# Reordering the border between the first 1x1 convolution and the Winograd 3x3 convolution of a bottleneck block

## The chip, the cores and the metric

The kernel runs on one core of one Trainium2 chip. The metric is the device time of one execution in microseconds; lower is better. All data are fp32.

## The reference

Two ResNet bottleneck blocks run one after the other on `x` of shape (64, 1024, 14, 14). A batch norm takes its mean and variance over the whole batch, so no normalised value exists before the last image of a convolution is done.

```python
def block(x, w1, ..., residual_scale):            # P = 256, Cout = 1024
    out = relu(bn(conv1x1(x, w1) + b1, g1, be1))   # 1024 -> 256
    out = relu(bn(conv3x3(out, w2) + b2, g2, be2)) # 256 -> 256, padding 1
    out = bn(conv1x1(out, w3) + b3, g3, be3)       # 256 -> 1024
    return relu(x + softplus(residual_scale) * out)
y = block(block(x, layer 0 weights), layer 1 weights)
```

## The kernel before, in words

`y_all` holds the 256 channels of the middle of a block in SBUF as two **slots** of 128 channels, for all 12544 pixels. The images are handled in 32 tiles `t` of two images (392 pixels).

**First convolution.** `Conv1` (L336) makes one unit of two tiles (in block 0) or of one tile (in block 1) as a Strassen-Winograd product: seven products `p1` to `p7` of four matmuls each instead of eight. The helper `matmul` (L171) issues every matmul in program order. `stream` (L303) interleaves the products of two consecutive units: `p1` of a unit, then `p4` and `p3` that are left over of the unit before, `p6`, `p5`, `p7`, and `p2`. Slot 1 of a unit is complete after its `p4` and `p7`, slot 0 after its `p2` and `p3`. Each result gets its bias and its `bn_stats` (L388, L391). In block 1 these products alternate with those of block 0's last convolution (`fused`, L1287).

**The border.** After the last `p4`, `one_done` (L1396) aggregates the statistics of slot 1, works out scale and shift in `affine` (L1345, a chain of small VectorE operations round one square root on ScalarE), and normalises slot 1 of the first image group on ScalarE (`norm`, L547). After the last `p3` the same is done for slot 0 (`first_norm`, L940). Then the 3x3 convolution may begin.

**3x3 convolution.** `conv2` (L557) works on 8 groups of 8 images, in one dimension as a Winograd transform with six products per group: pairs (1, 2), (3, 4) and (5, 0). `Inputs` (L603) makes the inputs of a pair on VectorE: row combinations `r` (L594, L683, L689, from a scratch tile `steps`, L700), then `sums` (L625), `v` (L631, with two edge columns on ScalarE, L636 and L637) and `diffs` (L641). Each of the 48 products needs three kinds of matmul, each of four instructions: `m` from `sums` and the filter `ua`, `l` from `diffs` and `ub`, and `columns` from `v` and `ub`, twice. `start` (L749) copies `m` from PSUM into the two halves EVEN and ODD of a `columns` bank pair on ScalarE (L759, L761), on which the `columns` matmuls accumulate; `middle` (L763) copies `l` as `ls` (L772, L774). VectorE adds both as `f` (L801). There are two `columns` pairs, two `l` and two `m` banks. The very first product has no `m` phase: its `sums` matmuls go straight into `columns`, slot 1 first.

The filters `ua` and `ub` are read from DRAM on SyncE's queue (L652). All tiles of `conv2` lie where tiles of the first convolution lay, and a pool waits for all that was in its place before.

The order within SyncE, VectorE and ScalarE is that of the tile scheduler, except where `keep_in_program_order` fixes it. All matmuls and all `act(...)` calls are so fixed; the edge columns, `ls` and the copies into `columns` are not.

The entry to the 3x3 convolution is in the code:

```python
        for banks in (columns(), columns()):
            n = MS * RT * GI * WH
            for q in (ODD, EVEN):
                matmul(banks[:, q, :n], ident, ident[:, :1].to_broadcast([P, n]), start=True, stop=True)
```

Those four matmuls multiply by the identity; nothing reads their result.

## Time and profile before

| | us |
|---|---|
| median of 3 executions (1924.05 to 1924.71) | 1924.67 |
| profiled execution | 1923.4 |
| its span, from first to last instruction | 1921.6 |
| TensorE matmul busy in it | 1903.4 (99%) |
| VectorE busy | 1546.8 (80%) |
| ScalarE busy | 1083.9 (56%) |
| GpSimd busy | 565.1 (29%) |

The profile is of one execution. In the timelines PE stands for TensorE, PEld for its weight loads, DVE for VectorE, ACT for ScalarE, POOL for GpSimd and SP for SyncE. Ends of matmuls are modelled, so the difference of two starts is a better duration than the one that is printed. An fp32 matmul appears as two records, so four matmuls are "x8". In a timeline line the columns are start, duration, engine, source line, operation, output and inputs, count, and in brackets the idle time before it with the instruction that ended it.

### The profile page before, as it was taken

What the parts mean: (1) busy time and instruction counts of PE and PEld (TensorE: products, weight loads), DVE (VectorE), ACT (ScalarE), POOL (GpSimd) and SP (SyncE); (2) the same over time, 40 slices, a digit from 0 to 9 for tenths busy, and PEclk for the clock granted to TensorE, in tenths of its full rate; (3) what the DMA queues carried; (4) which work ended last, traced back from release to release, by engine and by line L of the source; (5) the groups of instructions that cost most, each with busy time, mean ns of one, the idle gap of its engine ahead of it and who ended that gap; (6) DMA issues with size and microseconds to landing.
All of it is one profiled execution on the core that took longest, in us unless ns stands there. A gap on an engine that the chain in (4) does not pass through costs nothing.

```text
span 1921.6 us, 28727 instructions
## 1 busy us (share of the span) xinstructions
PE 1903.4 (99%) x10240; PEld 1597.4 (83%) x10240; DVE 1546.8 (80%) x2491; ACT 1083.9 (56%) x2148; POOL 565.1 (29%) x678
## 2 busy tenths in 40 slices
PE   9999999999999999999999999999999999999999
PEld 5555557999998799999999999989999987555555
DVE  5787767999998866776776767689999986888886
ACT  2222214677778355555555555556777682666665
POOL 0111100211204143433433333302121041666664
PEclk9999999999999999999999999999999999999999
DMA  7777644787856544444444444258778466889998
GB/s 286 271 251 274 220 153 142 199 225 211 211 178 170 189 161 171 169 168 176 179 182 168 168 168 177 125 166 208 222 208 223 142 171 242 290 326 346 325 344 300
DMA packets 198463, 408.77 MB, mean 213 GB/s; under 512 B 37040, under 2 KB 174960, under 8 KB 181808
## 3 DMA queue, kind: packets, MB, share of 16 engines
q1 hardware_dynamic: 159648, 321.84, 48.9%
q0 software_dynamic: 33056, 34.03, 8.6%
q10 hardware_dynamic: 5616, 51.06, 6.4%
q8 instruction: 81, 1.33, 0.3%
q14 instruction: 62, 0.51, 0.1%
HBM read 263.75 MB, written 115.34 MB: 197 GB/s over the span
## 4 chain that ended last, share of the span: by engine, by line
PE 92%; DVE 3%; DMA 1%; issue 1%; POOL 1%; ACT 1%; SPq 0%; DVEq 0%; ACTq 0%; POOLq 0%
PE cy L171 18%; PE ay L171 17%; PE columns L171 13%; PE cp L171 11%; PE ap L171 10%; PE m L171 7%; PE l L171 6%; PE cx L171 5%; PE ax L171 5%; PE ps L171 1%; DMA home<-y 1%; POOL home L1065 1%; DMA x<-in_x 0%; DVE v L631 0%; DVE sums L625 0%
## 5 line engine op out<-in xcount | busy, mean ns | idle before, releaser
L334 ACT ACTIVATE cu<-cy,scale 128x196 f32<-128x196 f32 (+1 forms) x552 | 256.3, 473 | 278.3 <-PE cy L171 272.9
L171 PE MATMUL columns<-v,ub 128*128 128x224 f32 (+1 forms) x1536 | 300.7, 337 | 0.0
L334 ACT ACTIVATE x<-x,shift 128x392 f32<-128x392 f32 x452 | 255.0, 613 | 72.6 <-POOL x L493 53.5
L171 PEld LDWEIGHTS columns<-v,ub 128*128 128x128 f32 x1536 | 269.3, 188 | 2.8
L467 DVE SCALAR_TENSOR_TENSOR x<-cp,scale,x 128x196 f32<-128x196 f32 (+1 forms) x368 | 178.1, 484 | 97.9 <-PE cp L171 96.5
L171 PE MATMUL cy<-ct,ws 128*128 128x196 f32 (+1 forms) x736 | 221.8, 383 | 1.2 <-ACT cu L334 1.2
L488 POOL TENSOR_TENSOR x<-x,cu 128x196 f32<-128x196 f32 (+1 forms) x184 | 159.9, 869 | 171.6 <-ACT cu L334 163.7
L171 PE MATMUL ay<-at,ws 128*128 128x196 f32 (+1 forms) x752 | 209.1, 381 | 0.0
L493 POOL TENSOR_TENSOR x<-x,cu 128x392 f32<-128x392 f32 x124 | 125.9, 1015 | 191.4 <-DVE x L467 191.4
L171 PEld LDWEIGHTS ay<-at,ws 128*128 128x128 f32 x752 | 136.5, 190 | 33.4
L171 PEld LDWEIGHTS cy<-ct,ws 128*128 128x128 f32 x736 | 133.4, 190 | 36.4 <-ACT cu L334 3.9
L171 PE MATMUL l<-diffs,ub 128*128 128x224 f32 (+1 forms) x768 | 149.1, 337 | 2.6 <-PE columns L171 2.6
L514 POOL TENSOR_TENSOR x<-x,cu 128x392 f32<-128x392 f32 x120 | 121.9, 1016 | 86.2 <-DVE x L467 65.3
L171 PE MATMUL m<-sums,ua 128*128 128x224 f32 (+1 forms) x752 | 145.9, 337 | 1.1 <-DVE sums L625 1.1
L334 ACT ACTIVATE au<-ay 128x196 f32<-128x196 f32 (+1 forms) x141 | 53.6, 380 | 155.4 <-PE ay L171 152.6
L171 PEld LDWEIGHTS l<-diffs,ub 128*128 128x128 f32 x768 | 134.3, 189 | 4.4 <-PE columns L171 3.9
L467 DVE SCALAR_TENSOR_TENSOR x<-cx,scale,x 128x196 f32<-128x196 f32 (+1 forms) x184 | 89.1, 484 | 56.7 <-PE cx L171 56.7
L171 PEld LDWEIGHTS m<-sums,ua 128*128 128x128 f32 x752 | 131.3, 189 | 2.9 <-DVE sums L625 2.5
L171 PE MATMUL cy<-y,w 128*128 128x196 f32 (+1 forms) x408 | 125.3, 393 | 0.0
L171 PE MATMUL cx<-y,w 128*128 128x196 f32 (+1 forms) x400 | 122.6, 391 | 0.0
L171 PE MATMUL cp<-y,ws 128*128 128x196 f32 (+1 forms) x368 | 113.6, 390 | 0.0
L761 ACT ACTIVATE columns<-m 128x448 f32<-128x448 f32 (+1 forms) x160 | 78.5, 490 | 59.5 <-PE m L171 57.0
(221 smaller groups left out, 3950.6 us busy)
## 6 DMA issues: line engine op xcount, KB each, us to landing
x<-in_x SPq DMA_DIRECT2D x62, 1568.0 KB, 6.8
ub<-u SPq DMA_DIRECT2D x94, 768.0 KB, 5.5
x<-mid SPq DMA_DIRECT2D x32, 1568.0 KB, 8.1
mid<-x ACTq DMA_DIRECT2D x31, 1568.0 KB, 5.1
out<-x SPq DMA_DIRECT2D x123, 392.0 KB, 5.5
ua<-u SPq DMA_DIRECT2D x94, 256.0 KB, 3.3
u<-y POOLq DMA_DIRECT2D x48, 256.0 KB, 5.6
home<-y SPq DMA_DIRECT2D x70, 96.0 KB, 3.7
```

The source lines that it names most:

```text
L171: tc.keep_in_program_order(nc.tensor.matmul(*args, **kw))
L334: tc.keep_in_program_order(nc.scalar.activation(*args, **kw))
L467: nc.vector.scalar_tensor_tensor(v, bank, self.scale[:, o : o + 1], v, ALU.mult, ALU.add)
L488: nc.gpsimd.tensor_add(self.part(1, 1), self.part(1, 1), u3)
L493: nc.gpsimd.tensor_add(v, v, self.u12)
L514: nc.gpsimd.tensor_add(v, v, self.u12[:, i * self.n : (i + 1) * self.n])
L761: nc.scalar.activation(v, m, AF.Copy)
L1065: ins = queue.dma_start(out=x[32 * i : 32 * i + 32, :, j], in_=y_all[32 * j : 32 * j + 32, :, a + i * run : a + i * run + run])
```

## The change

Four things are done at both borders. In the new code `late` is true in block 0, whose units have two tiles.

1. **The last `Conv1` unit gets an order of its own** (`closing`). `p4` of the last unit moves ahead of its `p2` and, in block 0, of the previous unit's `p3`. Both results of slot 1 then come earlier, and `p2` and `p3` of slot 0 come last. The last unit's `p5` bank is taken from the `ay` pair, its second saved product from another buffer. The summary of earlier statistics is made for each slot by itself.
2. **Slot 1's combinations begin before slot 0 is done.** `conv2` becomes a generator; `Border` advances it between the last products. The inputs of the first pair are made for each slot by itself (`first_combination`), nine small VectorE operations per slot, some of them placed inside slot 0's `affine` (`between`).
3. **The first matmuls are those of two products, slot 1 first**: the first product's `sums`, `l`, and `v`, then the second product's `m` and `l`, all for slot 1, then the same for slot 0. Two of the four identity matmuls are left.
4. **Buffers.** The x tiles are split into two pools of two, one of them on the right side of SBUF. That one is closed at the border, and a pool `early` takes its place for the first `r`, `v`, `sums`, `diffs` and `fa`. The first `ua` and `ub` get slots of their own, in block 0 over `at1` and `at2`, in block 1 over `w3`. The pools at the border and the PSUM pools wait for single tiles (`reuse_waits="tile"`). The loads of the second product's filters are split by slot.

`affine` loses one operation in the chain for one slot.

```diff
+        def closing(self, before):
...
+            yield from self.p1()
+            yield from before.p4()
+            summary(1)
+            if not late:
+                yield from before.p3()
+                summary(0)
+            yield from self.p6()
+            yield from self.p5()
+            yield from self.p7()
+            yield from self.p4()
+            border.affine_of(1)
+            border.norm(1)
+            if late:
+                yield from before.p3()
+                summary(0)
+            border.begin()
+            if late:
+                border.steps(1)
+            yield from self.p2()
+            if late:
+                border.steps(2)
+            yield from self.p3()
+            border.affine_of(0, lambda: border.steps(1 if late else 3))
+            border.norm(0)
+            border.steps(5 if late else 6)
...
-    def conv2(psum, pool, b, par, aff, affine_of, stats):
+    def conv2(b, par, aff, early, rest):
...
-        for banks in (columns(), columns()):
-            n = MS * RT * GI * WH
-            for q in (ODD, EVEN):
-                matmul(banks[:, q, :n], ident, ident[:, :1].to_broadcast([P, n]), start=True, stop=True)
...
+        def first_combination(x, s, t):
...
+            act(t[:, RT - 1], y_all[:, s, GPX - 2 * LINE : GPX], AF.Copy, scale=-3.0)
+            run(stt(t[:, :full], two_rows(0, s)[:, :, 0], -4.0, two_rows(0, s)[:, :, 1]))
+            yield
+            run(nc.vector.tensor_add(ra, t1, t2))
+            yield
+            x.add_columns(slice(0, 1), here)
+            yield
+            first, second = x.subtract_columns, x.step_columns
+            if s == 0:
+                first, second = second, first
+            first(slice(0, 1), here)
+            yield
+            second(slice(0, 1), here)
+            yield
+            run(nc.vector.tensor_sub(rb, t1, t2))
+            yield
+            x.add_columns(slice(1, 2), here)
+            yield
+            x.subtract_columns(slice(1, 2), here)
+            yield
+            x.step_columns(slice(1, 2), here)
+            yield
...
+        both_columns = EVEN, ODD
+        first.open()
+        second.open()
+        l, m, l2 = first.bank("l"), second.bank("m"), second.bank("l")
+        for s in reversed(range(MS)):
+            first.columns(*both_columns, slots=[s], sums=True)
+            if s:
+                first.part(l, DIFF, first.diffs, s)
+
+                n = MS * second.n
+                for q in both_columns:
+                    v = second.banks[:, q].rearrange("p o n -> p (o n)")
+                    matmul(v, ident, ident[:, :1].to_broadcast([P, n]), start=True, stop=True)
+            first.columns(*both_columns, slots=[s])
+            if s == 0:
+                first.part(l, DIFF, first.diffs, s)
+                first.middle(l)
+            second.part(m, SUM, second.sums, s)
+            if s == 0:
+                second.put(m)
+                long_work(0, 0)
+                finished.send(first)
+            second.part(l2, DIFF, second.diffs, s)
...
-        run(nc.vector.tensor_scalar(v, mv[:, :, 1], EPS, None, ALU.add))
+        run(nc.vector.tensor_scalar(v, mv[:, :, 1], EPS, -0.5, ALU.add, ALU.mult))
...
+        between()
         run(nc.vector.reciprocal(r, sd))
...
+                run(nc.vector.scalar_tensor_tensor(q[:, one], v[:, one], r[:, one], r[:, one], ALU.mult, ALU.mult))
+            run(nc.vector.tensor_mul(rg, r, par[:, g : g + n]))
```

## The prediction, put on record before the changed kernel ran

> **What bounds the kernel now.** I read the busy line of the page first, then TensorE's timeline for every gap, then VectorE and ScalarE round the gaps.

> ```profile
> PE 1903.4 (99%) x10240; PEld 1597.4 (83%) x10240; DVE 1546.8 (80%) x2491; ACT 1083.9 (56%) x2148; POOL 565.1 (29%) x678
> ```

> TensorE is busy for all but 18 us of the span, so only its gaps, and matmuls that do nothing, can be won. TensorE at the border of block 0, and the waits that follow:

> ```profile
> 301.45 2.80 PE L171 MATMUL ap<-x,ws 128*128 128x392 f32 x8
> 305.16 3.26 PE L171 MATMUL columns<-ident 128*128 128x448 f32 x8 [0.91 <-DVE y L388]
> 309.45 1.75 PE L171 MATMUL columns<-sums,ua 128*128 128x224 f32 x8 [1.03 <-issue]
> ...
> 320.16 1.69 PE L171 MATMUL columns<-v,ub 128*128 128x224 f32 x8
> 322.24 1.41 PE L171 MATMUL m<-sums,ua 128*128 128x168 f32 x8 [0.39 <-DVE sums L625]
> ...
> 347.80 1.75 PE L171 MATMUL l<-diffs,ub 128*128 128x224 f32 x8 [0.91 <-PE columns L171]
> ...
> 378.73 1.78 PE L171 MATMUL m<-sums,ua 128*128 128x224 f32 x8 [0.22 <-DVE sums L625]
> ...
> 382.45 1.75 PE L171 MATMUL l<-diffs,ub 128*128 128x224 f32 x8 [0.41 <-PE columns L171]
> ```

> The last product of the first convolution starts at 301.45 and, at 2.64 a product, ends at 304.1. The first useful matmul starts at 309.45: 5.3 us, of which 3.26 are identity matmuls. Then 0.39 + 0.91 + 0.22 + 0.41 = 1.93 us of waits follow, all on VectorE (the `diffs` before 347.80 and 382.45 end at 347.70 and 382.35); after that TensorE never waits again in this convolution. Block 1:

> ```profile
> 1255.46 1.49 PE L171 MATMUL ap<-x,ws 128*128 128x196 f32 x8
> 1258.77 3.26 PE L171 MATMUL columns<-ident 128*128 128x448 f32 x8 [1.82 <-DVE y L388]
> 1263.44 1.75 PE L171 MATMUL columns<-sums,ua 128*128 128x224 f32 x8 [1.42 <-issue]
> ...
> 1276.12 1.41 PE L171 MATMUL m<-sums,ua 128*128 128x168 f32 x8 [0.28 <-DVE sums L625]
> ```

> 6.7 us here, and later 0.28, 0.91, 0.21 and 0.41. VectorE in windows:

> ```profile
> 304.00:340.00 36.00, 33.67 (x182) 31.11 (x182) 34.68 (x51) 21.67 (x47) 0.14 (x2) 1.00 0.66 212
> 340.00:380.00 40.00, 38.87 (x220) 37.95 (x219) 38.72 (x50) 25.54 (x51) 6.41 (x6) 1.00 0.78 207
> ```

> The third number after the window's length is VectorE: 73.4 of 76 us. So **for 78 us after the border VectorE paces TensorE**; what TensorE wins at the border is kept only as far as VectorE is early too.

> ```profile
> 304.39 0.62 DVE L388 SCALAR_TENSOR_TENSOR y<-ap,par,au 128x392 f32<-128x392 f32 x1
> ...
> 309.73 0.85 DVE L594 SCALAR_TENSOR_TENSOR steps<-y 128x672 f32<-128x672 f32 x1
> ...
> 315.73 2.95 DVE L700 TENSOR_TENSOR steps<-y 128x2688 f32<-128x2688 f32 x1
> 318.79 1.63 DVE L594 SCALAR_TENSOR_TENSOR r<-steps 128x672 f32<-128x672 f32 x2
> ```

> and ScalarE, where the order of three rows will matter:

> ```profile
> 317.33 1.46 ACT L772 ACTIVATE ls<-l,par 128x224 f32<-128x224 f32 x4 [3.02 <-PE l L171]
> 318.84 1.09 ACT L761 ACTIVATE columns<-m 128x448 f32<-128x448 f32 x2
> 320.45 0.38 ACT L636 ACTIVATE v<-r 128x96 f32<-128x96 f32 x1 [0.52 <-DVE r L594]
> ```

> [...] in block 1 the result L388 of the last product ran only at 1258.20, after slot 1's whole `affine`, though its product ended at 1256.8. [...] for 224 and 448 elements, the rows show 0.39 and 0.62, so halving an operation costs something. [...] SyncE indeed stood until 305.09 for L388, and the first filter loads landed 2.3 us (`ua`, 128 KB) and 4.6 us (`ub`, 384 KB) later.

> **The change, part by part.** Durations are distances of starts in the trace before; orders are those in which the changed kernel's instructions stand on each engine.

> *Identity matmuls*: four become two, 1.63 us less per border, but the two left stand between useful ones and are no longer hidden.

> *Block 0, slot 1.* `p4` moves from 298.82 to 293.55, so slot 1's `affine` ends near 299.0 (5.27 earlier, and one operation of 0.19 less) and its normalisation (1.69) near 300.7. VectorE then does the previous unit's result and summary to 301.2, and `stt` (0.96), `r` (0.66) and `sums` (0.31) of slot 1 between the results of `p2` and `p3`. `sums` is ready at 304.45, so useful matmuls start at 304.55 instead of 309.45. The statistics chain of slot 0 hangs on `p3`, whose end doesn't move.

> *Block 0, VectorE after `p3`.* Of its work 0.96 + 0.66 + 0.31 = 1.93 us was done before; `diffs` fills the wait for the root (0.29); `affine` saves 0.19; the split costs about 0.08 each on four pairs and 0.31 on `r` (1.01 becomes 2 x 0.66), 0.6 in all. So L700 starts 1.9 us earlier (313.8), and the two `r` after it end at 318.5 instead of 320.4.

> *Block 0, TensorE.* From 304.55: `sums` 1.52, a wait for `diffs` to 306.5, `l` 0.76, identity 1.63, `v` 1.52, `m` 0.76, `l` 0.76, then slot 0 (its `sums` ready at 311.4) 1.52 + 1.52 + 0.76 + 0.76 + 0.76: done at 317.25. Next come the second product's EVEN matmuls, which need `columns<-m` from ScalarE. There **the two edge copies of the third product (128x96) now stand ahead of `ls` x4 and `columns<-m`**, and they need both `r` of 318.5. So 318.5 + 0.6 + 1.46 + 0.55 gives 321.2: TensorE waits 3.9 us, EVEN ends at 322.75, and the third product's `m` starts there, against 322.24 before: 0.5 later. `p3` to `m` contains the same 32 useful matmuls in both.

> *Block 0, afterwards.* The waits of 0.91, 0.22 and 0.41 were on VectorE, which is now 1.9 us early; its `diffs` before 347.7 also moves ahead of `fc` and the row outputs. They vanish: 1.54 - 0.5 = **1.0 us won**.

> *Block 1.* Products take 1.33. `p4` moves one product forward only, so `stt`, `r` and `sums` of slot 1 fall inside slot 0's `affine`, where they fill 0.52 of waiting; slot 0's shift comes at 1261.07 (before 1261.01). `sums` of slot 1 is ready at 1260.56 instead of 1263.23, L700 starts at 1268.2 (1.4 earlier). TensorE from 1260.65 by the same lengths: 1272.95. Here `ls` and the first `columns<-m` stand ahead of the edge copies: 1271.45 + 1.5 + 0.55 gives EVEN at 1273.6 and the third `m` at 1275.15, 0.97 earlier. At 1301.7 and 1332.6 VectorE decides: **1.4 us won**.

> *Edits at nothing.* The x pools hand out the same four places in the same order, and SyncE's sequence is the same except for the split. The filter loads: the first four can issue at 290, when `at2` is read for the last time, and the second `ub` at 301.5 after `p2`; with 4.6 us both are there before 306.5 and 311.2. If that cover is gone, see rival 2. The doubled issues on SyncE (about 0.5 each) delay only the third product's loads, needed at 322. The n=8 and n=2 `affine`s keep their length of chain.

> **Sum**: 1.0 + 1.4 = 2.4 us. The profiled execution would go from 1923.4 to 1921.0. The median lies 1.27 above it, so 1924.67 becomes **1922.3**, 0.12% less: by the 0.2% (3.9 us) that a measurement of this kernel can tell from no change, no difference. Unknown sizes: ScalarE's wait in block 0 is bounded below by 0.75 (`ls` and copy after the last `l`) and above by 4.5; the recovered waits by 0 and 1.54 per border.

> **Rivals.** *1, faster: ScalarE's order costs little and VectorE is the only limit.* For it: VectorE is 1.9 us early, and its 1.04 us idle at 359 (it waited for `columns`) can go too: 2.9 in block 0, 1.4 in block 1, so 4.3, 1920.4. [...] *2, the change doesn't do what it says: filters arrive as late as before.* Loads from 305 would put `ub` at 311, `l` at 311 instead of 306.5; part of it hides in ScalarE's wait; nothing is won, 1924.5. *3, slower: VectorE and ScalarE's order lock together.* TensorE's third `m` is now 4.25 after the two `r`. If the 1.9 us is not won (slot 1's work slips behind slot 0's statistics), they end at 321.0 with the split's 0.6, `m` starts at 325.3, and the other edge copies that now stand ahead of `columns<-m` in groups 0 and 1 keep the waits of 1.54: +3.1, and +1.2 in block 1: 1929.0. It decides from about 320.9 for the end of the two `r`; I work out 318.5.

> **How the numbers follow.** Main case 0.68 (1921.0 to 1924), rival 1 0.20, rival 2 0.04, rival 3 0.08. The range leaves out half of rival 3 and the far end of rival 1: 1919.4 to 1926.6. Beyond 0.2% faster is rival 1, 0.20; beyond 0.2% slower is rival 3 and a little else, 0.09; the rest 0.71.

> **What would show it.** Right: `columns<-sums` about 0.5 us after the last product; a wait of 3 to 4.5 us before the second product's EVEN matmuls in block 0 with ScalarE's 128x96 copies just before `ls`, and under 1 in block 1; no wait at what was 347.80; L700 1.4 to 1.9 us earlier after `p3`. Wrong: a long wait before the first `l` (filters), no wait before EVEN (rival 1), or new TensorE waits in groups 1 and 2 (rival 3).

## The result, and the profile after

The changed kernel takes **1928.69 us** (median of 13 executions, 1926.28 to 1930.15) against 1924.36 for the kernel before in the same session: ratio 1.0023, 95% interval 1.0015 to 1.0032. It is slower by 4.3 us, where 2.4 us less were forecast. Its profiled execution took 1928.93 us with a span of 1927.2, 5.6 more than before.

The busy line of its page:

```profile
PE 1905.0 (99%) x10232; PEld 1600.9 (83%) x10232; DVE 1547.5 (80%) x2509; ACT 1085.5 (56%) x2152; POOL 565.2 (29%) x678
```

TensorE has eight records less (two fp32 identity matmuls at each border), 3.26 us of work, and yet is busy for 1.6 us longer. So the same work is done more slowly somewhere. Windows of the kernel after show where (length, then busy time and count of PE, PEld, DVE, ACT, POOL, then PEclk, the granted clock of TensorE, DMA share and GB/s):

```profile
0.00:320.00 320.00, 315.54 (x970) 184.57 (x970) 229.50 (x327) 77.84 (x153) 26.83 (x56) 1.00 0.65 231
320.00:328.00 8.00, 5.48 (x22) 5.19 (x23) 6.86 (x8) 5.15 (x15) 0.00 (x0) 0.79 0.19 63
328.00:1261.00 933.00, 929.01 (x5909) 909.12 (x5907) 734.15 (x1357) 558.29 (x1171) 287.93 (x346) 1.00 0.54 179
1261.00:1269.00 8.00, 5.77 (x15) 4.89 (x16) 7.59 (x21) 3.64 (x11) 0.08 (x2) 0.57 0.66 223
1269.00:1930.00 661.00, 649.22 (x3319) 497.16 (x3318) 569.41 (x801) 440.62 (x806) 250.38 (x276) 1.00 0.79 250
```

The clock is 1.00 but for two stretches of 8 us, one at each border; in the kernel before it is 1.00 in all five windows. The timeline of TensorE at the border of block 0 in the kernel after (L175 is the old L171):

```profile
294.17 2.90 PE L175 MATMUL ay<-at,w 128*128 128x392 f32 x8 [0.59 <-ACT au L338]
...
304.89 1.78 PE L175 MATMUL columns<-sums,ua 128*128 128x224 f32 x8
307.15 1.00 PE L175 MATMUL l<-diffs,ub 128*128 128x224 f32 x4 [0.48 <-ACT sd L1452]
...
317.12 0.92 PE L175 MATMUL l<-diffs,ub 128*128 128x224 f32 x4
322.52 3.09 PE L175 MATMUL columns<-v,ub 128*128 128x224 f32 x8 [4.48 <-ACT columns L837]
325.40 1.72 PE L175 MATMUL m<-sums,ua 128*128 128x168 f32 x8
```

`columns<-sums` begins at 304.89, near the 304.55 of the forecast. Later comes a wait of 4.48 us, and after it eight rows that take 2.88 us from start to start where they took 1.53 before: nearly all of them at half speed. The third product's `m` starts at 325.40 instead of 322.24. From there to the end of this convolution TensorE does not wait once: the old waits of 0.91, 0.22 and 0.41 us are gone, and of the 3.16 us 1.66 are left when the next stage starts. Block 1:

```profile
1255.17 1.59 PE L175 MATMUL ay<-at,w 128*128 128x196 f32 x8 [0.42 <-ACT au L338]
...
1263.23 3.33 PE L175 MATMUL columns<-sums,ua 128*128 128x224 f32 x8 [3.81 <-issue]
1266.35 1.70 PE L175 MATMUL l<-diffs,ub 128*128 128x224 f32 x4
...
1279.33 1.81 PE L175 MATMUL columns<-v,ub 128*128 128x224 f32 x8 [1.19 <-ACT columns L837]
1280.97 1.30 PE L175 MATMUL m<-sums,ua 128*128 128x168 f32 x8
...
1305.77 1.75 PE L175 MATMUL l<-diffs,ub 128*128 128x224 f32 x8 [0.18 <-PE columns L175]
```

Here 3.81 us without a matmul are followed by half speed over `columns<-sums` (3.12 to the next start instead of 1.6) and `l` (1.49 instead of 0.76). `m` is 4.85 us later than before, 3.2 without what block 0 left over; the next stage starts 4.43 us later, so block 1 costs 2.8.

VectorE in block 0 did nearly what was forecast:

```profile
314.44 2.95 DVE L763 TENSOR_TENSOR steps<-y 128x2688 f32<-128x2688 f32 x1
317.50 1.63 DVE L640 SCALAR_TENSOR_TENSOR r<-steps 128x672 f32<-128x672 f32 x2
```

L763 (the old L700) starts 1.29 us earlier than before (1.9 forecast), and the two `r` end at 319.1. The chain of waits of the kernel after follows them (start, length, engine, what):

```profile
317.50 1.64 DVE r L640 x2
319.16 0.05 ACT v L682
...
319.44 0.35 ACT v L683
319.79 1.35 ACT ls L849 x4
321.14 0.43 ACT columns L837
321.57 0.46 ACT ls L851
322.03 0.44 ACT columns L837
322.48 0.04 issue
322.52 3.09 PE columns L175 x8
```

The edge copies stand ahead of `ls`, as forecast: `ls` starts only after them, though the `l` that it copies was done near 316.4, when the next matmuls start. But TensorE's EVEN matmuls wait for both copies `columns<-m`, EVEN and ODD, and a second `ls` lies between the two: 0.9 us that were not in the sum.

**Two readings of this.** Theory A: a wait of about 4 us costs a second time, because the clock falls in it or just after it and then stays at half for some us; in the kernel before, the identity matmuls in the wait ahead of `columns<-sums` had kept it up. Theory B: the waits are the whole loss. Beside that, which order (of ScalarE in block 0, of VectorE in block 1) makes the waits.

### The profile page after: what moved, and what is told of

It is laid out like the page before. It is cut to its first block, busy times and chain, and to the rows that moved or that the text cites. A ratio compares the mean times of both kernels' runs of the same rounds, so it can differ in the third digit from the quotient of the medians.

```text
span 1927.2 us, 28719 instructions
## 1 busy us (share of the span) xinstructions
PE 1905.0 (99%) x10232; PEld 1600.9 (83%) x10232; DVE 1547.5 (80%) x2509; ACT 1085.5 (56%) x2152; POOL 565.2 (29%) x678
## 3 DMA queue, kind: packets, MB, share of 16 engines
q8 instruction: 81, 1.33, 0.3%
## 4 chain that ended last, share of the span: by engine, by line
PE 95%; DVE 2%; DMA 1%; ACT 1%; issue 1%; POOL 0%; SPq 0%; DVEq 0%; ACTq 0%; POOLq 0%
PE ay L175 18%; PE cy L175 17%; PE columns L175 14%; PE cp L175 12%; PE ap L175 10%; PE m L175 7%; PE l L175 7%; PE cx L175 5%; PE ax L175 5%; PE ps L175 1%; DMA x<-mid 0%; DMA home<-y 0%; DMA x<-in_x 0%; POOL home L1160 0%; DVE v L677 0%
## 5 line engine op out<-in xcount | busy, mean ns | idle before, releaser
L175 PE MATMUL columns<-v,ub 128*128 128x224 f32 (+1 forms) x1536 | 303.7, 339 | 5.7 <-ACT columns L837 5.7
L175 PEld LDWEIGHTS columns<-v,ub 128*128 128x128 f32 x1536 | 270.0, 189 | 11.1 <-ACT columns L837 6.4
L175 PE MATMUL cy<-ct,ws 128*128 128x196 f32 (+1 forms) x736 | 221.8, 383 | 1.2 <-ACT cu L338 1.2
L175 PE MATMUL ay<-at,ws 128*128 128x196 f32 (+1 forms) x768 | 212.7, 382 | 0.0
L175 PEld LDWEIGHTS ay<-at,ws 128*128 128x128 f32 x768 | 139.3, 190 | 34.5
L175 PEld LDWEIGHTS cy<-ct,ws 128*128 128x128 f32 x736 | 133.4, 190 | 36.4 <-ACT cu L338 4.2
L175 PE MATMUL l<-diffs,ub 128*128 128x224 f32 (+1 forms) x768 | 150.4, 338 | 1.0 <-PE columns L175 0.6
L175 PE MATMUL m<-sums,ua 128*128 128x224 f32 (+1 forms) x752 | 146.3, 337 | 0.2 <-DVE sums L671 0.2
L175 PEld LDWEIGHTS l<-diffs,ub 128*128 128x128 f32 x768 | 134.9, 190 | 2.9 <-PE columns L175 1.2
L175 PEld LDWEIGHTS m<-sums,ua 128*128 128x128 f32 x752 | 132.1, 190 | 1.2 <-DVE sums L671 0.5
L175 PE MATMUL cy<-y,w 128*128 128x196 f32 (+1 forms) x408 | 125.3, 393 | 0.0
L175 PE MATMUL cx<-y,w 128*128 128x196 f32 (+1 forms) x400 | 122.6, 391 | 0.0
L175 PE MATMUL cp<-y,ws 128*128 128x196 f32 (+1 forms) x368 | 113.6, 390 | 0.6 <-DVE x L508 0.6
```

The lines of the kernel that those rows point to most:

```text
L175: tc.keep_in_program_order(nc.tensor.matmul(*args, **kw))
```

## The experiments

Executions of one kernel scatter over 2 to 6 us, so the traces are read by one length: from the first `columns<-sums` to the third product's `m`, the same 32 useful matmuls in every kernel.

| kernel | median, us | ratio to before (95%) | block 0: start, length | block 1: start, length |
|---|---|---|---|---|
| before | 1923.6 to 1924.4 | | 309.45, 12.79 | 1263.44, 12.68 |
| after | 1928.69 | 1.0023 (1.0015 to 1.0032) | 304.89, 20.51 | 1263.23, 17.74 |
| fill | 1923.59 | 0.9998 (0.9989 to 1.0006) | 305.36, 19.29 | 1262.19, 15.26 |
| act_order | 1924.46 | 1.0002 (0.9994 to 1.0010) | 305.09, 16.17 | 1261.11, 17.10 |
| late_b1 | 1926.94 | 1.0017 (1.0010 to 1.0024) | 304.93, 20.69 | 1263.40, 17.33 |
| all | 1924.09 | 1.0007 (0.9999 to 1.0015) | 304.74, 16.16 | 1261.31, 17.11 |
| order_fill | 1923.15 | 0.9998 (0.9990 to 1.0006) | 304.79, 16.18 | 1261.07, 15.45 |
| before_short_fill | 1927.50 | 1.0018 (1.0009 to 1.0026) | 309.44, 14.79 | 1264.89, 14.92 |
| put_first | 1922.40 | 0.9995 (0.9988 to 1.0001) | 304.58, 15.21 | 1260.40, 14.50 |
| late_full | 1923.50 | 0.9999 (0.9991 to 1.0007) | 304.73, 16.16 | 1259.71, 15.48 |
| combined | 1923.16 | 0.9999 (0.9991 to 1.0007) | 304.56, 15.22 | 1258.52, 14.53 |

(The kernel before took 1924.36, 1923.97, 1924.20 and 1923.59 us in the four sessions; each ratio is to its own session's.)

**fill.** Work without a use in the long waits.

```diff
+        if b == 1:                      # ahead of the first columns<-sums
+            for q in both_columns * 2:
+                v = first.banks[:, q].rearrange("p o n -> p (o n)")
+                matmul(v, ident, ident[:, :1].to_broadcast([P, n]), start=True, stop=True)
...
+        if b == 0:                      # ahead of the EVEN columns
+            v = psum.tile(448, "m")
+            for i in range(4):
+                matmul(v, ident, ident[:, :1].to_broadcast([P, 448]), start=True, stop=True)
```

> The changed kernel with four identity matmuls of 448 columns (about 3 us of TensorE) put into each of its two long TensorE waits: in block 1 into the first product's banks before its first matmul, in block 0 into a free bank between the second product's `l` and its EVEN columns. Nothing else is changed. Theory A (a wait of about 4 us costs a second time, because the granted clock falls after it): in block 1 the 8 rows columns<-sums take 1.7 us rather than 3.33 and the third product's m comes about 1.8 us earlier against the start of the border; in block 0 the EVEN columns<-v take 1.5 us rather than 2.88 and m comes 1.35 earlier; PEclk is 1.00 in both stretches; the time falls by about 3 us, to 1925.6. Theory B (the waits themselves are the whole loss and the lower clock only goes with them): m comes at the same times as in the changed kernel and the time stays at 1928.7.

TensorE in `fill`, block 0 and block 1:

```profile
318.35 3.18 PE L175 MATMUL m<-ident 128*128 128x448 f32 x8
323.00 1.81 PE L175 MATMUL columns<-v,ub 128*128 128x224 f32 x8 [1.47 <-ACT columns L837]
...
1262.19 1.78 PE L175 MATMUL columns<-sums,ua 128*128 128x224 f32 x8 [0.75 <-DVE sums L671]
```

and its windows there, with the granted clock (third number from the end) at 1.00 in both:

```profile
322.00:332.00 10.00, 9.00 (x57) 8.92 (x58) 9.52 (x10) 7.51 (x18) 0.00 (x0) 1.00 0.32 105
...
1256.00:1266.00 10.00, 9.25 (x39) 6.73 (x38) 9.08 (x30) 5.36 (x11) 0.15 (x2) 1.00 0.66 211
```

The useful matmuls still wait for the same rows of ScalarE and VectorE, yet they run at full speed when they start. The length falls by 1.22 us in block 0 and by 2.48 in block 1, the median from 1928.69 to 1923.59. Theory A. The 3.7 us of the two lengths are a little more than forecast (in block 1 `l` and the identity matmuls after it had been slow too); the rest of the 5.1 us between the medians is within their intervals.

**before_short_fill.** The other side: the kernel before, with its four identity matmuls read as bf16: 0.92 us for the four in block 0 of its trace, against 3.26 in fp32.

```diff
+                half = ident.bitcast(mybir.dt.bfloat16)
-                matmul(banks[:, q, :n], ident, ident[:, :1].to_broadcast([P, n]), start=True, stop=True)
+                matmul(banks[:, q, :n], half[:, :P], half[:, :1].to_broadcast([P, n]), start=True, stop=True)
```

> The kernel before with its four identity matmuls ahead of each 3x3 convolution taken in half-width numbers[...]. TensorE then has nothing to do from 305.9 to 309.45 (3.5 us) in block 0 and as long in block 1; nothing else is changed. Theory A (these matmuls keep the clock up): columns<-sums takes up to 3.3 us rather than 1.75 and the third m comes up to 2 us later in each block; the waits of 0.39, 0.91, 0.22 and 0.41 us that follow take up most of it, so the time is 1924.4 to 1927. Theory B (the clock has nothing to do with them): clock 1.000 and 1924.4.

TensorE in it, blocks 0 and 1:

```profile
305.15 0.92 PE L171 MATMUL columns<-ident 128*128 128x448 bf16 x4 [0.91 <-DVE y L388]
309.44 3.33 PE L171 MATMUL columns<-sums,ua 128*128 128x224 f32 x8 [3.37 <-DVE sums L626]
...
1264.89 3.33 PE L171 MATMUL columns<-sums,ua 128*128 128x224 f32 x8 [3.83 <-issue]
1268.01 2.86 PE L171 MATMUL columns<-v,ub 128*128 128x224 f32 x8
```

`columns<-sums` starts in block 0 when it did before and takes twice as long; `m` comes 2.0 and 2.2 us later against its start, and the kernel before loses **3.3 us** by doing less. That is above the top of what was expected (1927), because of the waits that follow only the one before `m` (0.39 and 0.28 us) was taken up: those of 0.90, 0.21 and 0.41 us stand in both blocks, and the next stage starts 1.86 us later after block 0 and 3.57 after both. In block 0 VectorE waited for ScalarE's `ls` (0.97 us) and then for TensorE's `columns` (0.94), and so came later itself.

**act_order.** ScalarE's rows at the border in program order, the edge copies last.

```diff
-                            nc.scalar.activation(v, m, AF.Copy)
+                            run_act(v, m, AF.Copy)           # act for the second product
-                            nc.scalar.activation(self.ls[:, q, o], l[:, o], AF.Identity, bias=bias, scale=sign)
+                            act(self.ls[:, q, o], l[:, o], AF.Identity, bias=bias, scale=sign)
+                edge = act if self.third else nc.scalar.activation
```

> The changed kernel with ScalarE's order fixed at the border: the first product's four ls, then the second product's two columns<-m, then the 128x96 edge copies of the third product. Theory A (ScalarE's order makes the 4.48 us wait in block 0, and the lower clock after it comes from that wait): ls can start at 317.9 at the latest, columns<-m end near 319.2, TensorE waits about 1 us, the EVEN columns take 1.5 us and the third m comes near 320.8 rather than 325.4; part of these 4.6 us is given back at the VectorE waits that return later in block 0, so the time falls by 3 to 4.6 us, to 1924.1 to 1925.7. Theory B (VectorE sets the border: its steps and r end at 319.1 whatever ScalarE does): the third m comes at 323 or later and the time falls by less than 2 us.

TensorE in it, block 0:

```profile
319.61 1.81 PE L175 MATMUL columns<-v,ub 128*128 128x224 f32 x8 [1.37 <-ACT columns L338]
321.26 1.30 PE L175 MATMUL m<-sums,ua 128*128 128x168 f32 x8
```

`m` comes 4.3 us earlier against the start: the wait is 3.1 us shorter, and the clock, which stays at 1.00 round the wait of 1.37 us (windows from 312 to 332), gives the other 1.2. VectorE's two `r` still end at 319.3, so ScalarE's order had made the wait, and VectorE was not the limit. The median falls by 4.2 us, though when the next stage starts only 2.2 of the 4.1 us at `m` are left: three waits, 1.2 us together, come back in between. Block 1 keeps its slow stretch.

**late_b1.** `p3` of the unit before moved behind `p4` in block 1.

```diff
-            if not late:
-                yield from before.p3()
-                summary(0)
...
-            if late:
-                yield from before.p3()
-                summary(0)
+            yield from before.p3()
+            summary(0)
```

> The changed kernel with the last-but-one unit's p3 (and slot 0's summary) in block 1 moved behind the last unit's p4, as block 0 has it. Theory A: slot 1's chain starts 1.33 us earlier, TensorE has 1.33 us more to do beside it, so that its wait of 3.81 us becomes 2.5 us; if the clock then stays at 1.00, the third m of block 1 comes 1.33 + 1.8 = 3.1 us earlier and the time is 1925.6; if 2.5 us are enough to lower the clock, only 1.3 us are won (1927.4). Theory B: slot 0's affine, which comes 0.6 to 1.3 us later, takes the place of slot 1's as what TensorE waits for, and nothing is won (1928.7).

TensorE's wait did not shrink to 2.5 us but grew to 4.33. VectorE in it:

```profile
1257.61 0.41 DVE L425 SCALAR_TENSOR_TENSOR y<-ap,par,au 128x196 f32<-128x196 f32 x1
...
1261.30 0.85 DVE L636 SCALAR_TENSOR_TENSOR t<-y 128x672 f32<-128x672 f32 x1
```

Slot 1 was normalised at 1259.41, but its first combination (L636) ran at 1261.30: `p3`'s result, the summary and slot 0's statistics now ran ahead of it on VectorE, from 1257.61 to 1261.30 without a pause. Neither theory holds as it was put: as in B the border wins nothing, but TensorE waits for slot 1's `sums` behind this work, not for slot 0's `affine`. The median is 1.75 us lower all the same. By the trace 0.24 us of that are there at `m` (the slow stretch lasts 3.4 us here instead of 6.8, which makes up for the longer waits), and the rest comes later in block 1's convolution, where the last three waits of the kernel after (0.75 us) are missing; no cause was sought.

**all.** act_order, late_b1 and `p7` ahead of `p5` in the last unit.

> The changed kernel with three edits: ScalarE's order fixed as in act_order, p3 late in block 1 as in late_b1, and p7 ahead of p5 in the last unit, so that p4 does not wait for the copy of its bank (waits of 0.59 and 0.42 us in the changed kernel). No filler matmul. If the three losses are separate: 1928.7 - 3.8 - 3.1 - 1.0 = 1920.8, below both kernels. If VectorE is what sets the borders once these are gone: near the kernel before, 1924.

The sum of the three gains, 1920.8, was missed by 3.3 us; the time is near the 1924 of the other branch. The late `p3` lost again as in late_b1 (a wait of 4.34), and the wait of `p4` only moved. TensorE in it:

```profile
288.74 5.53 PE L175 MATMUL ay<-at,ws 128*128 128x392 f32 x16 [0.59 <-ACT au L338]
294.12 2.80 PE L175 MATMUL ay<-at,w 128*128 128x392 f32 x8
```

`p6`, `p7` and `p4` accumulate in one bank, each copied out between; `p5` can stand in one gap only, and the other then waits 0.59 us.

**order_fill, order_fill2, order_fill1.** act_order with four, two and one identity matmuls in block 1 (the block 1 part of the first diff, with `both_columns * 2` cut to so many). Block 0 has only short waits in them (1.37 us at most), so a fall of the clock at a border is one at block 1's wait.

> act_order with the four identity matmuls of fill in block 1 only (block 0 has only a 1.37 us wait left, and gets none). If the two losses are separate (ScalarE's order in block 0, the granted clock in block 1): 1924.5 - 2.5 = 1922.0, faster than both kernels by about 2 us, clock 1.000. If the time is set elsewhere (act_order, fill and the kernel before all stand near 1924): no change, 1924.

> order_fill with two of the four identity matmuls: TensorE's wait in block 1 is cut from 3.82 us to about 2.3 us, still without work of its own. If only waits near 4 us lower the clock: columns<-sums takes 1.7 us, third m as in order_fill, 1922.0. If 2.3 us are enough: columns<-sums takes 3.2 us and the time is 1924.5, that of act_order.

> order_fill with one of the four identity matmuls: the wait is about 3.1 us. [...] If the clock looks at fixed windows that the wait may or may not fill, some executions show the lower clock and some not: time between 1922 and 1924.5, runs with clocks of both kinds.

TensorE in order_fill, order_fill2 and order_fill1:

```profile
1261.07 1.78 PE L175 MATMUL columns<-sums,ua 128*128 128x224 f32 x8 [0.75 <-DVE sums L671]
```

```profile
1261.06 3.35 PE L175 MATMUL columns<-sums,ua 128*128 128x224 f32 x8 [2.25 <-DVE sums L671]
```

```profile
1260.96 2.26 PE L175 MATMUL columns<-sums,ua 128*128 128x224 f32 x8 [3.02 <-DVE sums L671]
1263.02 1.70 PE L175 MATMUL l<-diffs,ub 128*128 128x224 f32 x4
```

| wait in block 1, us | kernel | median, us | executions with mean clock 1.000 |
|---|---|---|---|
| 0.75 | order_fill | 1923.15 | 13 of 13 |
| 2.25 | order_fill2 | 1924.75 | 5 of 12 |
| 3.02 | order_fill1 | 1924.03 | 3 of 12 |
| 3.82 | act_order | 1924.46 | 0 of 13 |

The mean is rounded, and it has a second source: the clock also falls after the last matmul of the kernel. In the trace of the kernel before that matmul ends at 1917.0 and the clock is 0.50 from 1919.91 on. The profiled execution of put_first below has 0.999, with 1.00 in the window up to 1917 and half clock in the last 2 us. So 1.000 says that block 1's wait did not lower the clock, 0.998 (2 executions of order_fill1, 3 of act_order) that it did, and 0.999 leaves it open; the kernel before, with waits of 1.82 and 1.42 us round its identity matmuls, had 1.000 in 112 and 0.999 in 24 of 136 executions. The profiled executions of the last three kernels of the table all show the fall at the wait. In order_fill2 the seven executions with 0.999 have a median 1.6 us above that of the five with 1.000, which is about what a fall costs, so most of the seven probably had one there.

When the clock changes is seen in windows of order_fill1:

```profile
1261.50:1262.00 0.50, 0.50 (x4) 0.50 (x3) 0.47 (x3) 0.21 (x1) 0.00 (x0) 1.00 1.13 299
1262.00:1263.00 1.00, 1.00 (x4) 0.92 (x4) 1.00 (x3) 1.00 (x1) 0.00 (x0) 0.56 1.03 352
...
1264.00:1265.00 1.00, 1.00 (x3) 0.78 (x3) 1.00 (x2) 0.06 (x1) 0.00 (x0) 0.50 0.38 137
1265.00:1266.00 1.00, 1.00 (x3) 0.52 (x2) 0.86 (x3) 0.21 (x2) 0.00 (x0) 0.73 0.01 2
```

Here the clock falls when TensorE has been working again for 1.2 us. At half speed a share of (1 - 0.56)/0.5 of the second window and (1 - 0.73)/0.5 of the last one passed, so the stretch runs from 1262.12 to 1265.54: 3.4 us. In order_fill2 it is 3.4 us too, but begins at 1260.88, before the matmuls. Both lose 1.6 to 1.7 us at `m`, half of it. The same kernel shows executions of both kinds, so the length of the wait alone does not decide (see the last section). order_fill itself gained less than expected on act_order (1.3 instead of 2.5; by its trace 1.65).

**put_first, put_first_p7, late_full, combined.** What is left of the waits: ScalarE's two `columns<-m` ahead of `ls`, on top of order_fill; then `p7` ahead of `p5`; `late = True` in both blocks; and all of it.

```diff
                 first.part(l, DIFF, first.diffs, s)
-                first.middle(l)
...
                 second.put(m, act)
+                first.middle(l)
```

> order_fill with ScalarE's two columns<-m of the second product ahead of the first product's four ls. The wait of 1.37 us before the EVEN columns should go to about 0.3 us (m is done 0.8 us after l, the two copies take 1.1 us). If ScalarE still sets the border: third m 1.0 us earlier in each block (near 320.0 and 1275.5) and 1921.2 to 1922. If VectorE sets it (sums of the third product end near 320.0 whatever ScalarE does, or waits return later in the block): third m near 320.2, and the time stays at 1923.15.

> put_first with p7 ahead of p5 in the last unit, so that p4 does not wait for the copy of its bank: 0.59 us of TensorE's waits in block 0 and 0.42 us in block 1 go, and slot 1's chain starts that much earlier. If the chain through slot 1 sets the border: 1.0 us less than put_first. If the work of VectorE sets it: the same as put_first within 0.4 us.

> order_fill with block 1 in the order of block 0: p3 of the unit before after p4, and slot 1's combination started before p2 (late_b1 had moved only p3, and slot 1's first combination then stood behind slot 0's summary and results on VectorE). Slot 1's sums come about 0.9 us earlier, slot 0's affine about 0.9 us later. If slot 1 sets when TensorE begins and TensorE is the limit after that: columns<-sums of block 1 near 1260.1 and 0.9 us won (1922.3). If VectorE's whole work is the limit: nothing, or up to 0.9 us lost (1923.2 to 1924).

> put_first_p7 and late_full together. If their gains add: 1920 to 1921, below the kernel before by 3 to 4 us. If VectorE's work is the limit: as order_fill, 1923.

TensorE in put_first, block 0:

```profile
318.14 1.81 PE L175 MATMUL columns<-v,ub 128*128 128x224 f32 x8 [0.42 <-ACT columns L338]
319.79 1.38 PE L175 MATMUL m<-sums,ua 128*128 128x168 f32 x8
...
346.30 1.75 PE L175 MATMUL l<-diffs,ub 128*128 128x224 f32 x8 [1.25 <-issue]
```

The wait goes from 1.37 to 0.42 and `m` comes 1 us earlier against the start; in block 0 a wait of 1.25 us ahead of an `l` then takes part of it back. put_first has the lowest median of all, 1922.40, far below the changed kernel; against the kernel before its ratio is 0.9995 with an interval that just reaches 1, so a gain is not shown. put_first_p7 (1922.84, ratio 0.9997) won nothing, since its wait only moves. late_full starts 1.36 us earlier than order_fill in block 1 and is ahead by 1.33 at `m`, but by 0.09 when the next stage starts (1540.56 against 1540.65). combined is 3.07 us ahead of the kernel before at block 1's `m` and 1.84 at the next stage; its median, 1923.16, does not show it. So what is won at `m` is largely lost again before the next stage. In put_first VectorE is busy for 74.0 of the 76 us after block 0's border (73.4 before), which fits the prediction's view that it paces TensorE there. That it does so alone is not shown: in before_short_fill VectorE waited for the others in its turn.

## Why the prediction was wrong

It said 1922.3, and its range ended at 1926.6. Point by point:

- **"TensorE waits 3.9 us to 321.2."** This is the step that failed most. The wait was seen and named, with its cause, but it was priced as a wait only: the sum has no term for the clock, and all matmuls after the wait stand in it at full speed. The wait measured 4.48 us, and the clock after it added 1.22 us in block 0 (fill). In block 1 the prediction itself left TensorE empty from 1256.8 for 3.85 us, measured 3.81, and the clock added 2.48. These two terms are 3.7 us, where the sum of all gains was 2.4. In the windows of order_fill1 the clock is 0.50 in a stretch of 3.4 us; in order_fill2 a step of that length with 2.07 us without a matmul was followed by one at half clock (last section).
- **"Identity matmuls: four become two, 1.63 us less per border."** They were counted as work that goes. In block 1 they had stood in the wait ahead of `columns<-sums`: four of them put back there keep the clock at 1.00 (fill, order_fill). In the kernel before, cutting them to 0.92 us with nothing else changed costs 3.3 us (before_short_fill). In block 0 of the changed kernel the long wait is a new one at another place, which ScalarE's order makes (act_order).
- **The EVEN matmuls.** The prediction had them start after one `columns<-m`; they wait for both, with an `ls` between: 0.9 us (the chain above); what makes them wait for both was not separated. The order of the edge copies was read rightly, and undoing it brings `m` 4.3 us forward (act_order).
- **`p4`.** It was put at 293.55 with no wait; in both blocks it waits for the copy of its bank, 0.59 and 0.42 us, and with it slot 1's chain and L763 (314.44 instead of 313.8).
- **Third `m`:** 322.75 forecast in block 0, 325.40 measured; in block 1, without the 1.77 us by which it began later, 1275.15 and 1279.20.
- **"Afterwards: the waits vanish."** Right in block 0, all 1.54 us, but in part by luck: `m` starts 3.16 us later than before, so the inputs had that much more time. Where it starts 0.98 us earlier (act_order), waits of 1.18 us are back. In block 1 0.18, 0.18 and 0.39 us are left of 1.53.
- **The rivals.** Rival 2 is out: the first `l` waits 0.48 us, for `diffs` that end at 307.05. Rival 3 named nearly the measured time, 1929.0, by luck and not by its cause: its condition, the two `r` ending after 320.9, was not met (319.1). Rival 1 (no cost of ScalarE's order) is out: with that order changed `m` comes 4.3 us earlier (act_order).
- **What the mechanism is worth.** With ScalarE's order fixed and the clock kept up (order_fill), the next stage starts 0.88 us earlier than before in block 0 and 0.92 after both blocks. So of the 1.0 and 1.4 us that were forecast block 0's came and block 1's did not: there the two identity matmuls that are left (1.5 us) and the 1.37 us of ScalarE's copies use up the earlier start. These are single traces; the medians show no difference from the kernel before (ratio 0.9998, interval 0.9990 to 1.0006).

Left open: about 1.2 us of the 5.6 arise after block 1's convolution. Some 0.9 of them lie in the stage that follows (61.9 us from its first matmul to `cx<-y,w` before, 62.8 after); in the other kernels here that length runs from 61.3 to 62.8 without an edit in it, so no cause is named.

## What to carry to other kernels

Before matmuls without a use are taken out, look at the wait that they would leave. In these runs a wait of 2.25 us and more could be followed by half speed for 3.4 us or more (order_fill2), and with matmuls put into such a wait the third product's `m` came 1.22 and 2.48 us sooner against the start of the border (fill). Where TensorE waits for a copy, find out what stands ahead of that copy on its engine, and fix the order where the scheduler chooses it. The wait between two accumulations into one bank was moved, not removed, by exchanging the products around it.

## What the runs showed of the hardware

**Steps of the clock.** In these traces the granted clock changes in steps of 3.4 us, also while matmuls run: in the kernel after, the window of block 0 gives (1 - 0.79)/0.5 x 8 = 3.4 us and that of block 1 6.9, one and two steps. Cut at the changes, its trace shows it at the second digit (TensorE's busy time is the second number after the window):

```profile
319.41:322.83 3.42, 0.31 (x2) 0.31 (x3) 3.42 (x4) 3.42 (x10) 0.00 (x0) 1.00 0.63 216
322.83:326.24 3.41, 3.41 (x11) 3.14 (x10) 2.93 (x4) 1.51 (x5) 0.00 (x0) 0.50 0.00 0
326.24:329.65 3.41, 3.41 (x23) 3.37 (x23) 2.05 (x3) 2.46 (x4) 0.00 (x0) 1.00 0.27 79
...
1258.08:1261.49 3.41, 1.34 (x9) 1.03 (x7) 3.06 (x14) 2.38 (x4) 0.15 (x2) 1.00 0.42 101
1261.49:1264.91 3.42, 1.68 (x5) 1.57 (x6) 3.19 (x11) 1.38 (x4) 0.00 (x0) 0.50 0.99 326
1264.91:1268.32 3.41, 3.41 (x10) 2.98 (x9) 3.24 (x8) 1.68 (x6) 0.00 (x0) 0.50 0.50 187
1268.32:1271.73 3.41, 3.41 (x16) 2.67 (x15) 3.38 (x8) 0.50 (x3) 0.00 (x0) 1.00 0.00 0
```

The clock falls at 322.83 and 1261.49, 938.66 us or 275 steps of 3.413 us from each other, and all changes within one of the profiled executions lie a whole number of such steps apart. So each execution can be cut into its steps, and the time without a matmul counted in each.

```profile
1256.74:1260.15 3.41, 1.68 (x11) 1.38 (x11) 2.27 (x12) 1.10 (x3) 0.00 (x0) 1.00 0.00 0
1260.15:1263.56 3.41, 0.91 (x4) 0.28 (x4) 2.69 (x11) 2.62 (x4) 0.15 (x2) 1.00 0.50 128
...
1257.46:1260.87 3.41, 1.34 (x4) 0.38 (x2) 3.18 (x9) 2.23 (x5) 0.15 (x2) 1.00 0.77 233
1260.88:1264.29 3.41, 3.23 (x9) 2.94 (x10) 3.27 (x13) 2.41 (x5) 0.00 (x0) 0.50 1.02 333
```

The first pair is from before_short_fill: 1.73 us of 3.41 are idle, the clock stays at 1.00 in this step, and it falls only after the next one, which has 2.50 idle. The second is from order_fill2: 2.07 us are idle, and the next step runs at half clock. A step at half clock with 1.33 us or more idle was followed by another (3 cases; 1.73 from 1261.49 in the kernel after), one with 0.46 or less by full speed (none idle from 1264.91).

**What follows for a wait.** Where the wait lies against the steps decides, and that differs from execution to execution. The wait of 2.25 us lowered the clock in some executions and not in others, and one execution of the kernel after, with a mean clock of 0.999, cannot have had a fall at both of its long waits; the waits in order_fill, 1.37 us and less, lowered it in none of 13. Falls cost 1.2 to 2.5 us per border after the wait had ended. No count of waits shows this: TensorE is 99% busy in the changed kernel, and the mean clock of the whole span, 0.997 instead of 1.000, is the one figure that points to it.
